# A decoder layer on one core: the value products moved to the end of each fused group, their copies to the start of the next, routing operands in PSUM, and two sums moved up

## The chip, the cores and the metric

The kernel runs on one core of a Trainium2 chip. It is written by hand for five engines that each work through their own instructions in order: TensorE (PE, matrix products and transposes), VectorE (DVE), ScalarE (ACT), GpSimd (POOL) and SyncE (SP, which here only issues transfers). An instruction starts when the one before it on its engine is through and the semaphores it waits for have been raised. The metric is the time on the device of one execution, in microseconds (us), median of several runs.

## The reference

Sixteen sequences of 256 tokens with 256 channels pass through a decoder layer with three residual blocks, each closed by a layer norm; all is float32.

```
x = _layernorm(x + attn(x, w_fc, w_proj, ln_g, ln_b))        # square of relu(scores), 4 heads
x = _layernorm(x + xattn(x, ctx, ctx, frac, ...))            # 16 heads of 16 channels
x = _layernorm(x + ffn(x, gate_W, gate_b, wi, wo, lora ...))

# xattn
logits = einsum('bhqd,bhkd->bhqk', Q, K) * scale
D = clip(frac[:, None, :] - frac[:, :, None], -0.2, 0.2)
attn = gamma * logits + delta * (ap * max(D, 0) + an * min(D, 0))
out = einsum('bhqk,bhkd->bhqd', softmax(attn), V) ; out @ Wo.T + bo

# ffn: one expert of eight per token, experts differ by a rank-4 addition
top1 = argmax(softmax(x @ gate_W.T + gate_b))
inter = relu(x @ wi.T + wi_b + (x @ lora_A[i].T) @ lora_B[i].T)    # i = top1
out = inter @ wo.T + wo_b
```

## The kernel before

The first 252 us are the first attention. Then the cross attention runs in N = 64 groups n: group n holds batch n//4 and four of its sixteen heads. The loop `for n in range(N + 2)` works on three groups at a time: `now` is group n, `last` is n-1, `older` is n-2. Its order of statements is the order on the engines; nothing rearranges it.

What a group goes through:

- `logits` (L664, PE): 32 products add the logits to the positive bias that ACT put into the four banks `ps_l` (`positive`, L654).
- `maxima` (L682, DVE): eight instructions add the negative bias, which POOL made (L642), and take each row's maximum.
- From n = 14 on the groups are *direct*: two of the four head blocks are exponentiated in place (`exp_rows`, L696, ACT), turned in 32x32 blocks by DVE (`blocks`, L707), written to DRAM (`away_z`) and read back in turned form into `pT` (`fetch`, L724). The other two have their maxima subtracted on POOL (`subtract`, L733), are turned by PE (`turned`, L743) and exponentiated by ACT (`exps`, L750).
- `attend` (L764, PE, 16 products) multiplies `pT` by the values, with a column of ones that gives the sums. It is done for `older`, two iterations after the logits. Two groups share one PSUM bank, `batch.av`, which is the single buffer of tag V in `psV` (`bufs=1`).
- `keep` (L777, DVE) copies that bank to `raw` when its second half is done, so for every other group; after every second copy `gather` lets SP issue the transfer of the sums (L574) and of the values (`away_v`, L579). `regroup` (L585), `invert` (reciprocal of the sums, L593), `spread` and `divide` follow one or two iterations on.

Each iteration also does one large piece and one small one of the projections: queries (L477), keys (L503), values (L532), output (L614), and the transposes of the next input (L464, `small_piece`, one iteration in four).

From n = FIRST = 15 on, the expert FFN of 512 earlier rows at a time is woven in: `tb, part = divmod(n - 15, 8)`, FUSED = 6 blocks of rows, so six cycles of eight parts. Part 0 turns the rows (L857, copies L860), part 1 computes the gates (L872, copy L882 on ACT), part 2 routes (`route`, L887 to L909, DVE) and parts 2 and 3 do the first FFN product (`inner`, L945) and the low-rank addition (`lora`, L958; L967 and L971 evict it), with `turn_um` (L919) in part 2. Parts 4 to 7 do the second product, one quarter each (`finish`: `outer`, L978, 16 products; then `add`, L991, and its statistics L191, L192, DVE). Parts 5 and 7 are called `apart`: their L978 goes into the bank of tag V, which the value products use too. So the products of parts 5 and 7 are left until the start of the part after, where 32 of them stand together behind the logits. In parts 2 and 3 (`halved`) the 16 products stand after `lora`.

`now.later` is true in parts 0 and 1, where the transposes of L707 are put off to the next part. `tile_b()` hands out three PSUM banks in turn (tags B, B, W); a transposition or product that takes a bank waits for the reader of what it held three hand-outs before.

Of the kernel before, what the change touches and what calls it, by code (L numbers as in the profile page):

```python
# [9 lines left out]
FP = mybir.dt.float32  # L10
AF = mybir.ActivationFunctionType
ALU = mybir.AluOpType
AX = mybir.AxisListType

P = 128
# [7 lines left out]
def tile_decoder_layer(ctx: ExitStack, tc: tile.TileContext, a: dict, out: bass.AP):  # L23


    nc = tc.nc
# [9 lines left out]
    E = a["gate_b"].shape[1]  # L36
# [9 lines left out]
    small = ctx.enter_context(tc.tile_pool(name="small", bufs=4))  # L46
# [3 lines left out]
    def tile_b():  # L50

        if turns:
            turns[0] += 1
            if turns[0] % 3 == 0:
                return psV.tile([P, 512], FP, tag="W", name="ps_b")
        return psB.tile([P, 512], FP, tag="B", name="ps_b")

    def tile_v(tag="V"):
        return psV.tile([P, 512], FP, tag=tag, name="ps_v")
# [6 lines left out]
    rev = const.tile([P, 4, E], FP, name="rev")  # L66
# [138 lines left out]
    def newton(mv, near, n):  # L205

        t = small.tile([P, n], FP, tag="sd", name="sd")
        nc.vector.scalar_tensor_tensor(t, mv[:, :, 1], EPS, near, ALU.add, ALU.mult)
        nc.vector.scalar_tensor_tensor(t, t, -0.5, near, ALU.mult, ALU.mult)
        rs = small.tile([P, n], FP, tag="rs", name="rs")  # L210
        nc.vector.scalar_tensor_tensor(rs, t, 1.5, near, ALU.add, ALU.mult)
        return rs
# [214 lines left out]
    if True:  # L427
# [357 lines left out]
        groups = [Group(batches[n // 4], n % 4) for n in range(4 * B)]  # L785
        N = len(groups)
# [19 lines left out]
        def step(piece):  # L806
            if piece:
                next(piece, None)
# [3 lines left out]
    if True:  # L812
        out_view = out.rearrange("(b j p) c -> b p j c", j=4, p=P)

        class Block:
# [68 lines left out]
            def route(self):  # L884
                ps = tile_b()
                for j in range(2):
                    nc.tensor.transpose(  # L887
                        ps[:, j * P : (j + 1) * P], self.gT[:, j * P : (j + 1) * P], ident
                    )

                gp = ps[:, 0 : 2 * P].rearrange("p (j t w) -> p t j w", j=2, t=2)
                lg = small.tile([P, 4, E], FP, tag="lg", name="lg")
                nc.vector.tensor_tensor(
                    lg.rearrange("p (t j) e -> p t j e", t=2), gp[:, :, :, 0:E],
                    gateb.rearrange("p (t j) e -> p t j e", t=2), ALU.add,
                )
                top = small.tile([P, 4, 1], FP, tag="top", name="top")
                nc.vector.tensor_reduce(top, lg, AX.X, ALU.max)

                hot = small.tile([P, 4, E], FP, tag="hot", name="hot")  # L900
                nc.vector.tensor_tensor(hot, lg, top.to_broadcast([P, 4, E]), ALU.is_ge)
                nc.vector.tensor_tensor(hot, hot, rev, ALU.mult)
                first = small.tile([P, 4, 1], FP, tag="first", name="first")
                nc.vector.tensor_reduce(first, hot, AX.X, ALU.max)
                nc.vector.tensor_tensor(hot, hot, first.to_broadcast([P, 4, E]), ALU.is_equal)

                self.um = small.tile([P, 4, 4, E, R], FP, tag="um", bufs=1, name="um")
                for j in range(4):
                    nc.vector.tensor_tensor(  # L909
                        self.um[:, j],  # L910
                        gp[:, j // 2, j % 2, E:W].rearrange("p (e r) -> p e r", r=R).unsqueeze(1).to_broadcast([P, 4, E, R]),
                        hot[:, j].unsqueeze(1).unsqueeze(3).to_broadcast([P, 4, E, R]),
                        ALU.mult,
                    )
# [98 lines left out]
    with tc.manual_schedule():  # L1013
# [15 lines left out]
        first = batches[0]  # L1029
# [8 lines left out]
        for tb in range(NB):  # L1038
# [16 lines left out]
            if tb > 2:  # L1055
                older = rows_in[tb - 3]
# [70 lines left out]
        FUSED, FIRST = NB - 2, 15  # L1127
# [26 lines left out]
        for n in range(N + 2):  # L1154
            now, nxt, last, older = (
                groups[n + d] if 0 <= n + d < N else None for d in (0, 1, -1, -2)
            )
            large_piece, small_piece, more = pieces(n)
            tb, part = divmod(n - FIRST, 8)
            ff = rows_out[tb] if 0 <= tb < FUSED or (tb == FUSED and part < 2) else None  # L1160
            halved = ff and part in (2, 3)
# [4 lines left out]
                done = rows_out[tb - 1]  # L1166

            apart = 0 <= tb < FUSED and part in (5, 7)
            b, og = divmod(n, 4)

            if n < 2:
# [7 lines left out]
                six.keep_gates()  # L1179
            if n > N:  # L1180
                six.inner(0, range(0, 1))
            if older and not halved and not apart and n != N:
                if 0 <= n - 1 - FIRST < 8 * FUSED and (n - 1 - FIRST) % 8 in (5, 7):
                    groups[n - 3].attend()
                older.attend()
            if last and last.direct:
                last.room()
                if not last.later:
                    last.fetch()
# [25 lines left out]
            if halved:  # L1215
                for g in range(2, 4) if last.direct else range(2):
                    last.turned(g)
                    last.exps(g)
                if part == 2:
                    ff.route()  # L1220
                if now.direct:
                    for g in range(2):
                        now.exp_rows(g)
                now.subtract((nc.gpsimd, nc.vector))
                if now.direct:
                    now.blocks()
                if part == 2:
                    ff.biased()
                if done:
                    done.ready(newton(done.mv, done.near, 4))  # L1230
                ff.inner(part - 2, range(0, 3))
                if part == 2:
                    ff.turn_um()
                ff.inner(part - 2, range(3, 4))
                ff.lora(part - 2, scalar=(0,))
                for g in range(4):
                    nxt.positive(g)
                older.attend()
            else:


                eager = n in (12, 13, 14)
                if n >= N or not now.direct:
                    acts = "e0 s0 s1 e1 s2 s3" if eager else "s0 s1 g e0 s2 e1 s3"
                    if ff and part == 0:
                        acts = "s0 s1 g e0 e1 s2"
                else:
                    acts = "s0 s1 g s2 s3" if last.direct else "s0 e0 s1 e1 s2 s3"
                    if part != 0 or not ff:
                        acts += " x0 x1"  # L1250
                for act in acts.split():
                    g = int(act[1:] or 0)
                    if act == "g":
                        if ff and part == 1 and n < N:
                            ff.keep_gates()
                    elif act[0] == "s":
                        if act == "s3" and n == N:
                            older.attend()
                        if nxt:
                            nxt.positive(g)  # L1260
                    elif act[0] == "x":
                        if now:
                            now.exp_rows(g)
                    elif last:
                        if last.direct:
                            g += 2
                        last.turned(g)
                        last.exps(g)
            if older:
                older.keep()  # L1270
            if n == 0:
                for piece in (outs[0], early[3], outs[1]):
# [25 lines left out]
                prep.rows()  # L1298
            if done and not halved:
                done.ready(newton(done.mv, done.near, 4))  # L1300
            if now and now.direct and not halved and not now.later:
                now.blocks()
            if ff and part >= 4:
                ff.finish(part - 4, tile_v() if apart else None)
            if last and (not last.direct or now and now.direct and not halved):
                for g in range(2, 4):
                    last.turned(g)
# [2 lines left out]
                step(large_piece)  # L1310
            step(small_piece)
            step(small_piece)
            if last and last.direct and last.later:
                last.fetch()
            if n == N:
# [117 lines left out]
```

## Time and profile before

| | |
|---|---|
| median of 3 runs | 887.87 us (887.59 to 888.99) |
| profiled execution | 887.49 us, span 885.7 us |
| granted TensorE clock | 0.999 |
| POOL busy | 466.6 us, 53% of the span |
| POOL waits (the longest in the loop): L733 for the maxima | 84.3 us, 40 waits |
| ACT, L967 for `lora` | 68.3 us, 16 waits |

"Span" is the time from the first to the last instruction that the profiler recorded; the rest of the execution lies around it. A line of the timeline gives the start of a run of like instructions, the time from the start of the first to the end of the last, the engine, the source line, the operation, what it writes and reads, the shape, how many there are, and in brackets the idle time just before, with what ended it. Busy times of consecutive matrix products overlap a little, as they are pipelined; from the start of one group to the start of the next is the truer length. In the chain of waits, each piece is followed back to what released it.

A cycle of eight parts takes some 77 us: the logits of part 1 start at 428.66, 506.48, 583.09, 659.71 and 736.33; the cycle that is looked at most closely here has its logits of parts 4 to 7 at 617.90, 627.16, 634.46 and 643.63 and of the following cycle's parts 0 to 3 at 650.93, 659.71, 666.36 and 680.90.

### The profile page before, as it was taken

To read this page: it belongs to the slowest core of one execution; us is meant where nothing else is said; L and a number is where in the kernel's file an instruction comes from. 1 tells how busy PE (TensorE), PEld (TensorE's weight loads), DVE (VectorE), ACT (ScalarE), POOL (GpSimd) and SP (SyncE) were. 2 spreads that over 40 slices of the span, in tenths; PEclk is the share of its full clock that TensorE was granted. 3 is DMA by queue.
4 is the path that set the end of the run, shared out by engine and by line. 5 is a ranking of instruction groups with operands and counts; after the bars stand their busy time and mean duration, and the time that the engine had idled before them with its cause. 6 is when DMAs were issued, how large, how long until landed. Compare 5 with 4: busy or idle time off the path is not lost.

```text
span 885.7 us, 20853 instructions
## 1 busy us (share of the span) xinstructions
PE 862.4 (97%) x7708; PEld 513.1 (58%) x7708; DVE 693.3 (78%) x1975; ACT 577.0 (65%) x1012; POOL 466.6 (53%) x455
## 2 busy tenths in 40 slices
PE   8999999999999999999999999999999999999997
PEld 4334444444456776567547656754765675576655
DVE  6878899889779898769778877877887787777444
ACT  5766777777788788647747765774875577475111
POOL 1100223322479898656828765883976678374010
PEclk9999999999999999999999999999999999999999
DMA  5501101010001333454454536445453644642001
GB/s 139 159 1 43 54 24 44 31 49 1 8 8 48 99 98 110 139 162 149 158 155 150 158 129 184 151 155 168 138 164 133 193 151 135 181 149 102 28 7 41
DMA packets 70373, 92.94 MB, mean 105 GB/s; under 512 B 13824, under 2 KB 55296, under 8 KB 70272
## 3 DMA queue, kind: packets, MB, share of 16 engines
q1 hardware_dynamic: 69696, 91.35, 33.2%
q8 instruction: 61, 1.00, 0.5%
q14 instruction: 40, 0.33, 0.1%
q10 hardware_dynamic: 576, 0.26, 0.1%
HBM read 50.43 MB, written 39.58 MB: 102 GB/s over the span
## 4 chain that ended last, share of the span: by engine, by line
PE 44%; DVE 11%; issue 2%; POOL 1%; ACT 1%; DMA 0%; ACTq 0%; POOLq 0%; DVEq 0%
PE ps_l L945 9%; PE ps_b L978 6%; PE ps_l L664 5%; PE ps_v L764 5%; PE ps_b L743 4%; DVE neg L682 3%; PE ps_b L614 3%; PE ps_v L978 3%; PE ps_b L477 2%; PE ps_l L958 2%; DVE z L707 1%; PE ps_b L503 1%; PE ps_b L532 1%; POOL neg L733 1%; DVE dpos L547 1%
## 5 line engine op out<-in xcount | busy, mean ns | idle before, releaser
L682 DVE CUSTOM_DVE_ANT_0 neg<-ps_l,neg 128x256 f32<-128x256 f32 x512 | 181.5, 420 | 41.4 <-PE ps_l L664 38.3
L642 POOL TENSOR_SCALAR neg<-dneg,aneg,delta 128x512 f32<-128x512 f32 x252 | 198.9, 804 | 20.9 <-PE ps_b L743 10.0
L654 ACT ACTIVATE ps_l<-dpos,apos_d 128x512 f32<-128x512 f32 x256 | 172.2, 688 | 49.9 <-DVE mx L682 30.9
L354 DVE TENSOR_TENSOR pr<-pr 128x1024 f32<-128x1024 f32 x128 | 153.8, 1243 | 30.2 <-ACT pr L353 29.8
L733 POOL TENSOR_TENSOR neg<-neg,mx 128x1024 f32<-128x1024 f32 x65 | 124.0, 1909 | 85.4 <-DVE mx L682 84.3
L353 ACT ACTIVATE pr<-ps_a 128x1024 f32<-128x1024 f32 x128 | 125.0, 1026 | 53.0 <-PE ps_a L345 52.7
L345 PE MATMUL ps_a<-xnT,kT 64*64 64x512 f32 x1024 | 124.6, 593 | 1.0 <-ACT xnT L330 0.4
L364 PE MATMUL ps_v<-pr,vv 64*64 64x512 f32 x1024 | 122.7, 589 | 0.0
L945 PE MATMUL ps_l<-xt,wi 128*128 128x512 f32 x248 | 111.7, 596 | 0.2
L750 ACT ACTIVATE pT<-ps_b 128x512 f32<-128x512 f32 x160 | 87.4, 590 | 32.4 <-PE ps_b L743 30.9
L743 PE MATMUL ps_b<-ident,neg 128*128 128x128 f32 x640 | 87.1, 277 | 3.4 <-ACT pT L750 2.3
L743 PEld LDWEIGHTS ps_b<-ident,neg 128*128 128x128 f32 x640 | 71.5, 141 | 24.0 <-issue 6.2
L364 PEld LDWEIGHTS ps_v<-pr,vv 64*64 64x64 f32 x1024 | 45.0, 133 | 64.5 <-issue 54.6
L379 POOL TENSOR_TENSOR xt<-xt,half 128x512 f32<-128x512 f32 x15 | 19.1, 1274 | 119.8 <-ACT half L378 119.8
L419 POOL TENSOR_TENSOR hid<-hid,bo 128x256 f32<-128x256 f32 x32 | 43.6, 1366 | 71.8 <-ACT hid L251 71.8
L696 ACT ACTIVATE neg<-neg,mx 128x256 f32<-128x256 f32 x192 | 81.3, 498 | 0.0
L764 PE MATMUL ps_v<-pT,vaug 128*32 128x256 f32 x1024 | 74.3, 385 | 7.2 <-DVE x L991 6.0
L664 PE MATMUL ps_l<-kM,qT 32*64 32x256 f32 x2048 | 79.8, 388 | 0.0
L345 PEld LDWEIGHTS ps_a<-xnT,kT 64*64 64x64 f32 x1024 | 41.9, 133 | 65.3 <-issue 52.5
L945 PEld LDWEIGHTS ps_l<-xt,wi 128*128 128x128 f32 x248 | 45.6, 191 | 49.4 <-issue 44.6
L978 PE MATMUL ps_b<-wof,hT 128*128 128x256 f32 x304 | 68.4, 380 | 0.0
L524 POOL TENSOR_SCALAR kM<-keys,of_head 128x512 f32<-128x512 f32 x22 | 38.7, 1760 | 48.4 <-DVE keys L513 48.4
(137 smaller groups left out, 1183.3 us busy)
## 6 DMA issues: line engine op xcount, KB each, us to landing
pT<-away_z SPq DMA_DIRECT2D x192, 128.0 KB
away_z<-z SPq DMA_DIRECT2D x24, 512.0 KB
away_z<-kT SPq DMA_DIRECT2D x24, 512.0 KB
away_v<-raw SPq DMA_DIRECT2D x16, 512.0 KB
cT<-in_ctxT SPq DMA_DIRECT2D x16, 256.0 KB
v<-away_v SPq DMA_DIRECT2D x32, 128.0 KB
invs<-rows SPq DMA_DIRECT2D x16, 256.0 KB
x<-in_x SPq DMA_DIRECT2D x7, 512.0 KB
```

The source lines that it names most:

```text
L345: nc.tensor.matmul(sc[64 * k : 64 * k + 64, h, :], lhsT=kT[64 * h : 64 * h + 64, q, hf * P + 64 * k : hf * P + 64 * k + 64], rhs=self.xnT[ ...
L353: nc.scalar.activation(pr, sc, AF.Relu)
L354: nc.vector.tensor_tensor(pr, pr, pr, ALU.mult)
L364: nc.tensor.matmul(self.acc[k][64 * h : 64 * h + 64, :], lhsT=vv[64 * k : 64 * k + 64, hf, 64 * q : 64 * q + 64], rhs=pr[64 * k : 64 * k + ...
L642: nc.gpsimd.tensor_scalar(self.neg[:, g], self.batch.dneg, aneg[:, h : h + 1], delta, ALU.mult, ALU.mult,)
L654: nc.scalar.activation(banks[g], self.batch.dpos.rearrange("p j k -> p (j k)"), AF.Copy, scale=apos_d[:, h : h + 1],)
L664: nc.tensor.matmul(banks[g][64 * h : 64 * h + 64, j * S : (j + 1) * S], lhsT=self.batch.qT[rows, self.o, j * P + 64 * h : j * P + 64 * h + ...
L682: nc.vector.tensor_tensor_reduce(out=self.t[:, g, j, :], in0=banks[g][:, j * S : (j + 1) * S], in1=self.neg[:, g, j, :], scale=-1.0 if min ...
L733: eng.tensor_tensor(rows, rows, top.to_broadcast([P, 4, S]), ALU.subtract)
L743: nc.tensor.transpose(ps[:, k * S + j * P : k * S + (j + 1) * P], self.t[:, g, j, k * P : (k + 1) * P], ident,)
L945: nc.tensor.matmul(self.banks[g], lhsT=wi[:, c, f * P : (f + 1) * P], rhs=self.xT[:, c, :], start=(c == 0), stop=False,)
L978: nc.tensor.matmul(ps[:, 0:C], lhsT=self.hT[f][:, j * P : (j + 1) * P], rhs=wof[:, f, :], start=(f == 0), stop=(f == FC - 1),)
```

## The change

- **Values last.** For n = 15 to 63, `older.attend()` no longer stands behind the logits (or behind `lora` in parts 2 and 3): it is the last thing of the iteration, after the large and the small piece. Putting off the products of parts 5 and 7 to the following part falls away.
- **Copies first.** `keep` of those groups goes to the start of the following iteration, behind the logits and before the maxima, the fetch and the regrouping: `groups[n - 3].keep()`.
- **Some sums first.** In parts 5 and 7 `ff.finish`, with its addition and statistics on DVE, stands ahead of `now.blocks()`, the transposition on DVE.
- **Routing operands in PSUM.** `lg` and the intermediate masks (`held`) lie in free columns of the bank that the gates were turned into; only the final mask `hot` lies in SBUF. The number of instructions of each engine stays the same.

```diff
                 gp = ps[:, 0 : 2 * P].rearrange("p (j t w) -> p t j w", j=2, t=2)
-                lg = small.tile([P, 4, E], FP, tag="lg", name="lg")
+                lg = ps[:, 2 * P : 2 * P + 4 * E].rearrange("p (j e) -> p j e", e=E)
+                held = ps[:, 3 * P : 3 * P + 4 * E].rearrange("p (j e) -> p j e", e=E)
...
-                nc.vector.tensor_tensor(hot, lg, top.to_broadcast([P, 4, E]), ALU.is_ge)
-                nc.vector.tensor_tensor(hot, hot, rev, ALU.mult)
+                nc.vector.tensor_tensor(held, lg, top.to_broadcast([P, 4, E]), ALU.is_ge)
+                nc.vector.tensor_tensor(held, held, rev, ALU.mult)
                 first = small.tile([P, 4, 1], FP, tag="first", name="first")
-                nc.vector.tensor_reduce(first, hot, AX.X, ALU.max)
-                nc.vector.tensor_tensor(hot, hot, first.to_broadcast([P, 4, E]), ALU.is_equal)
+                nc.vector.tensor_reduce(first, held, AX.X, ALU.max)
+                nc.vector.tensor_tensor(hot, held, first.to_broadcast([P, 4, E]), ALU.is_equal)
...
             apart = 0 <= tb < FUSED and part in (5, 7)
+            lastly = FIRST <= n < N
...
-            if older and not halved and not apart and n != N:
-                if 0 <= n - 1 - FIRST < 8 * FUSED and (n - 1 - FIRST) % 8 in (5, 7):
-                    groups[n - 3].attend()
+            if older and not lastly and n != N:
                 older.attend()
+            if FIRST < n <= N:
+                groups[n - 3].keep()
             if last and last.direct:
...
                 ff.lora(part - 2, scalar=(0,))
                 for g in range(4):
                     nxt.positive(g)
-                older.attend()
...
-            if older:
+            if older and not lastly:
                 older.keep()
...
+            if apart:
+                ff.finish(part - 4, tile_v())
             if now and now.direct and not halved and not now.later:
                 now.blocks()
-            if ff and part >= 4:
-                ff.finish(part - 4, tile_v() if apart else None)
+            if ff and part >= 4 and not apart:
+                ff.finish(part - 4)
...
             step(small_piece)
             step(small_piece)
+            if lastly:
+                older.attend()
             if last and last.direct and last.later:
                 last.fetch()
```

The lines of the kernel after are those of the kernel before plus one from L893 on, and shifted by a few more in the loop.

## The prediction

> **What bounds the kernel now.** I read the busy times first, then the list of waits, then the timelines of single engines in one cycle.
>
> ```profile
> PE 862.4 (97%) x7708; PEld 513.1 (58%) x7708; DVE 693.3 (78%) x1975; ACT 577.0 (65%) x1012; POOL 466.6 (53%) x455
> ```
>
> PE is the bound on average, with 3% idle. So values that only change places gain at most the places where PE waits, and they lose wherever they were filling a wait. The waits with a value product behind them are short:
>
> ```profile
> PEld ps_v L764 <- DVE x L991: 11.1, 12, 2.1
> ...
> PE ps_v L764 <- DVE x L991: 6.0, 6, 1.6
> ```
>
> Six waits of PE on the sum L991 make 6.0 us, about one per cycle, in part 0:
>
> ```profile
> 649.96 1.04 PE L743 MATMUL ps_b<-ident,neg 128*128 128x128 f32 x8
> 650.93 1.12 PE L664 MATMUL ps_l<-kM,qT 32*64 32x256 f32 x32
> 652.83 2.65 PE L764 MATMUL ps_v<-pT,vaug 128*32 128x256 f32 x32 [0.78 <-DVE x L991]
> ```
>
> Here 32 products wait 0.78 us and then take 2.65 us where part 6's take 1.86 (635.51 to 637.38), the second half waiting for ACT's exponentials: 0.78 + 0.79, about 1.5 us of idle PE. Part 1 has 1.87 for 16 products where 1.00 is usual (0.8 idle), part 2 has 0.52 before L919. Together 2.8 us a cycle. The sum L991 is late because DVE is full in parts 6 and 7; its timeline there has no gap over 0.4 us from 635.91 on:
>
> ```profile
> 648.62 1.72 DVE L547 CUSTOM_DVE_ANT_1 dpos<-frow,nfcol 128x512 f32<-128x512 f32 x1
> ...
> 651.14 0.16 DVE L246 SCALAR_TENSOR_TENSOR nm<-mv,rs 128x4 f32<-128x4 f32 x1
> 651.22 1.25 DVE L707 STREAM_TRANSPOSE z<-neg 128x1024 f32<-128x1024 f32 x1
> 652.39 0.38 DVE L991 TENSOR_TENSOR x<-x,ps_v 128x256 f32<-128x256 f32 x1
> ```
>
> In part 4 the end is set by ACT, while PE has the values to do:
>
> ```profile
> 619.43 1.07 PE L764 MATMUL ps_v<-pT,vaug 128*32 128x256 f32 x16
> 620.43 1.99 PE L532 MATMUL ps_b<-wv,cT 128*128 128x256 f32 x8
> 622.26 3.62 PE L978 MATMUL ps_b<-wof,hT 128*128 128x256 f32 x16
> 625.72 1.04 PE L743 MATMUL ps_b<-ident,neg 128*128 128x128 f32 x8
> 626.59 0.64 PE L464 MATMUL ps_b<-ident,hid 128*128 128x128 f32 x4
> 627.16 1.12 PE L664 MATMUL ps_l<-kM,qT 32*64 32x256 f32 x32
> ...
> 620.55 2.76 ACT L654 ACTIVATE ps_l<-dpos,apos_d 128x512 f32<-128x512 f32 x4 [2.21 <-PE ps_v L764]
> 623.25 1.69 ACT L696 ACTIVATE neg<-neg,mx 128x256 f32<-128x256 f32 x4
> 624.84 0.59 ACT L251 ACTIVATE hid<-hid,nm,rs 128x256 f32<-128x256 f32 x1
> 626.35 1.08 ACT L750 ACTIVATE pT<-ps_b 128x512 f32<-128x512 f32 x2 [0.92 <-PE ps_b L743]
> ```
>
> ACT is free at 625.43 and waits 0.92 us for the transposes; PE hardly waits.
>
> **The change, part by part.** Everything is a replay by hand of the cycle shown, each instruction with the duration it has there, in the order and with the waits of the program after.
>
> *Part 4.* The values (1.00) leave the front, so L532 starts at 619.43, L978 at 621.26, L743 at 624.72 and ends at 625.6. L464 takes the third bank in turn, which the second exponential reads. ACT's chain does not move: it starts from the maxima, which start from the logits, and is free for L750 at 625.43; its two end at 626.5. L464 (0.53 of PE time) runs to 627.0, the values 1.00 to 628.03: that is when part 5's logits start, instead of 627.16, **+0.87**. PE has 0.9 us of new idle time, which the values covered. Lower bound: 0, if L464 started right behind L743 (625.6); upper bound: if the exponentials end where they do now (627.44), 628.97, +1.8. I take 0.87. L464 stands in part 4 of five cycles.
>
> *Parts 5 and 6.* The sum L991 now precedes the transposition L707 on DVE, so part 5's values find their bank free at once: the logits of part 6 start at 635.46 with 16 values already done (+1.0, then -1.0 within part 6, since all products are only moved). But maxima of part 6 start 0.84 later (636.74). The copy (0.69) leaves this stretch, 638.67, yet little is won by it: L547 behind it takes 1.33 us because it ends with POOL's L733, which starts when the maxima end, and L547 takes 0.68 where POOL does nothing. DVE's stretch ends at 645.4 instead of 644.6.
>
> *Part 7.* The copy comes first here: 645.35 to 646.05, maxima from 646.0 (before: 644.91). Behind: the reciprocal, keys, L547 held by POOL's L733 until about 651.3, the four small steps to 652.3, the sum L991 to 652.7. PE itself is through with L978 and L743 at 651.07; the values want the bank that L991 reads, and so wait from 651.07 to 652.75. They end at 653.75, when the logits of part 0 start, instead of 650.93: +2.8. Queued behind this wait on PE are those logits, and behind them all of part 0. On SP the sums and `away_v` go out 1.3 us before the fetch (its 4 issues 1.74) and the regrouping waits for `away_v` to land (4.3 us from issue to landing: 641.78 to 646.04); the sums take 2.6 us and land near 648.7, just when the reciprocal's turn comes. Price 0; if they are late, all they are late by, up to 0.6.
>
> *Part 0.* The 32 products and their waits are gone (650.93 to 655.41 was 4.48 for 1.05 of logits). Maxima from 655.03, ACT's positives to 658.68 (+0.9 behind the maxima, 2.76 long), then ACT's copies L860 to 659.7. PE is ready for L464 before, but its bank waits for the second copy: 659.8 to 660.3, values to 661.3. That is part 1's logits: **+1.6** (before: 659.71).
>
> *Parts 1 and 2.* The 0.8 of part 1 is won: part 2's logits at 667.17 (+0.8). L945 starts at 669.55 (+1.0). The routing, from DVE's L893 to L905, takes 2.4 us now, with two-operand steps stretched by POOL's L865:
>
> ```profile
> 671.60 0.15 DVE L893 TENSOR_TENSOR lg<-ps_b,gateb 128x32 f32<-128x32 f32 x1
> 671.78 0.18 DVE L898 TENSOR_REDUCE top<-lg 128x4 f32<-128x32 f32 x1
> 672.00 0.60 DVE L901 TENSOR_TENSOR hot<-lg,top 128x32 f32<-128x32 f32 x1
> 672.64 0.65 DVE L902 TENSOR_TENSOR hot<-hot,rev 128x32 f32<-128x32 f32 x1
> ```
>
> L893, with one operand in PSUM, takes 0.15. With L901, L902 and L905 (0.43) at 0.15 to 0.2 each, some 1.2 us go. Then L919 starts behind L945 without its 0.52 wait: 669.55 + 5.32 = 674.87 against 674.45, **+0.42** per crossing. If the operands bring nothing, the wait stays and it is +0.9. The trace has 0.19 for L901 with POOL idle, so below 0.15 each there is nothing to expect.
>
> [...]
>
> *Sum.* Five crossings, five parts 4: 5 x (0.87 + 0.42) = 6.45. First cycle, whose part 0 loses a filled wait before any gain from part 7: +0.5 (bounds 0 and 0.87). Last crossing, where no L464 stands behind and PE waits 1.63 us for L991: -0.3 (bounds -1.6 and 0). +6.6 on the profiled 887.49 is 894.1; the median lies 0.4 above that execution. I predict 894.0.
> With all bounds: part 4 from 0 to +1.8, crossing from -0.5 (the gain at L919 stays, the rest is regained in part 0) to +1.6, so 5 x -0.5 - 1.6 = -4 to 5 x 3.4 + 0.9 = +18; halfway to each, the likeliest case's own range is 889 to 899.
>
> **Rivals.**
> 1. *The waits go, and nothing takes their place* (faster). Place: parts 7 to 2. It decides if L991 of part 7 ends before 651.07, when PE is ready. For it: L991 is 1.25 earlier relative to L707. Against it: the maxima before it start 1.1 later and L547 is held by POOL. Price: all 2.8 us in six cycles give -17, 871; with part 4's loss of 4.4 it is 875. If only part 7's crossing comes out even and the routing's 0.52 goes in each of six cycles, 884.8. Chance 0.24; I see it between 875 and 886.
> 2. *Even* (no change). Part 4's +0.87 is taken up by DVE's slack (1.24 us idle before the maxima at 628.44) and the crossing gives +-0.4. Against: PE has no slack behind part 4. 886 to 889.7, chance 0.11.
> 3. *SP falls behind* (slower still). The regrouping at the head of part 7 holds SP until `away_v` has landed; if the turned blocks of part 7 go out behind it, the values of part 1 wait. From an SP delay of about 2 us on it shows, some 0.6 to 1.5 us a cycle: 897 to 903. Against: away_z of part 7 follows L707, at 654. Chance 0.10.
> My forecast: 0.55.
>
> A measurement of this kernel can tell 0.2%, 1.8 us, from no change. Faster 0.24, same 0.11, slower 0.65. The range 882.5 to 900 leaves out the deep end of rival 1 and half of rival 3.
>
> **What would show it.** Right: PE's wait before L764 on L991 (part 7) grows to some 1.7 us while those of part 0 go; part 4 shows 0.9 idle before L464; no wait on L909 before L919; L901, L902 near 0.2. The cycle is 77.9 instead of 76.6. Wrong: the cycle at or below 76.6; L991 in part 7 done before the transposes end; or new waits on the fetched `pT`, which I priced at nothing.

## The result and the profile after

| | median | against the kernel before |
|---|---|---|
| kernel before | 887.73 us (887.58 to 888.99, 4 runs) | |
| kernel after | 894.42 us (893.47 to 894.87, 4 runs) | 1.0065, 95% interval 1.0053 to 1.0078 |
| profiled execution after | 894.21 us, span 892.5 us | span 6.8 us longer |

The forecast was 894.0. The busy times of the page are nearly those of before (PE 858.5 instead of 862.4 us), so the kernel after has no more work to do; PE stands still longer. The list of waits of the kernel after says where (engine, tile and line that waits, what it waits for: total us, times, longest):

```profile
PEld ps_v L764 <- DVE x L992: 11.5, 6, 2.3
...
PE ps_v L764 <- DVE x L992: 9.9, 6, 2.0
...
PE ps_b L743 <- DVE vaug L540: 6.4, 6, 2.1
...
PE ps_b L464 <- ACT pT L750: 3.8, 5, 0.9
```

The waits on the sum (now L992) have not gone but grown from 6.0 to 9.9 us, and two new ones have come. The 2.6 us before the transposes of um are off the list. How long each part of a cycle takes, from its logits to those of the next part, in the same two executions (n is the group, the third cycle from n = 35 on; all by the starts of L664 on PE's timeline):

| part (n) | 4 (35) | 5 (36) | 6 (37) | 7 (38) | 0 (39) | 1 (40) | 2 (41) | 3 (42) | sum |
|---|---|---|---|---|---|---|---|---|---|
| before | 9.26 | 7.30 | 9.16 | 7.30 | 8.79 | 6.65 | 14.53 | 13.62 | 76.61 |
| after | 10.18 | 8.30 | 8.30 | 9.89 | 7.57 | 5.86 | 13.61 | 13.63 | 77.34 |

The cycle with part 4's logits at 621.89 shows the two places. PE's timeline in part 4:

```profile
628.71 1.04 PE L743 MATMUL ps_b<-ident,neg 128*128 128x128 f32 x8
630.49 0.66 PE L464 MATMUL ps_b<-ident,hid 128*128 128x128 f32 x4 [0.74 <-ACT pT L750]
631.08 1.07 PE L764 MATMUL ps_v<-pT,vaug 128*32 128x256 f32 x16
632.08 1.12 PE L664 MATMUL ps_l<-kM,qT 32*64 32x256 f32 x32
```

and ACT's:

```profile
628.84 0.59 ACT L251 ACTIVATE hid<-hid,nm,rs 128x256 f32<-128x256 f32 x1
629.35 1.08 ACT L750 ACTIVATE pT<-ps_b 128x512 f32<-128x512 f32 x2
```

PE has finished L743 and stands until ACT's second exponential has let go of the bank; the values, which had covered this, stand behind. Part 7 on PE, on DVE and on POOL:

```profile
651.56 3.62 PE L979 MATMUL ps_v<-wof,hT 128*128 128x256 f32 x16
655.01 1.04 PE L743 MATMUL ps_b<-ident,neg 128*128 128x128 f32 x8
657.56 1.07 PE L764 MATMUL ps_v<-pT,vaug 128*32 128x256 f32 x16 [1.52 <-DVE x L992]
658.57 1.12 PE L664 MATMUL ps_l<-kM,qT 32*64 32x256 f32 x32
...
654.50 1.72 DVE L547 CUSTOM_DVE_ANT_1 dpos<-frow,nfcol 128x512 f32<-128x512 f32 x1
...
657.10 0.41 DVE L992 TENSOR_TENSOR x<-x,ps_v 128x256 f32<-128x256 f32 x1
...
653.77 1.90 POOL L733 TENSOR_TENSOR neg<-neg,mx 128x1024 f32<-128x1024 f32 x1 [2.52 <-DVE mx L682]
```

1.52 us of wait for L992, with the logits queued behind it. And the routing on DVE, whose rows stood at 0.60 and 0.65 before:

```profile
677.24 0.17 DVE L894 TENSOR_TENSOR ps_b<-ps_b,gateb 128x32 f32<-128x32 f32 x1
...
677.67 0.20 DVE L902 TENSOR_TENSOR ps_b<-ps_b,top 128x32 f32<-128x32 f32 x1
677.90 0.20 DVE L903 TENSOR_TENSOR ps_b<-ps_b,rev 128x32 f32<-128x32 f32 x1
```

One thing was not foreseen at all. In the first two cycles the wait of part 7 is 2.04 us, and the windows of the kernel after show what follows (stretch, length, then busy us and instructions of PE, PEld, DVE, ACT and POOL, then the granted TensorE clock, DMA share, GB/s):

```profile
418.00:420.00 2.00, 1.94 (x13) 1.52 (x12) 1.59 (x6) 2.00 (x6) 1.81 (x1) 1.00 0.94 291
420.00:422.00 2.00, 0.02 (x3) 0.02 (x4) 1.86 (x7) 0.84 (x3) 2.00 (x2) 1.00 0.60 133
422.00:424.00 2.00, 2.00 (x32) 1.00 (x40) 1.71 (x3) 2.00 (x5) 2.00 (x4) 0.69 0.29 89
424.00:426.00 2.00, 2.00 (x26) 1.09 (x11) 0.68 (x3) 0.67 (x2) 1.07 (x2) 0.50 0.73 294
426.00:428.00 2.00, 2.00 (x13) 1.71 (x13) 2.00 (x13) 1.78 (x3) 0.00 (x0) 0.96 0.03 9
```

Behind an idle stretch from 420 to 422 the clock goes to 0.50, and it is back, at 0.96, in the stretch from 426 on; the logits in between take 2.01 us where 1.12 is usual.

### The profile page after: what moved, and what is told of

Read it like the earlier page. It is cut to its first block, busy times and chain, and to the rows that moved or that the text cites. A ratio compares the mean times of both kernels' runs of the same rounds, so it can differ in the third digit from the quotient of the medians.

```text
span 892.5 us, 20853 instructions
## 1 busy us (share of the span) xinstructions
PE 858.5 (96%) x7708; PEld 510.1 (57%) x7708; DVE 687.5 (77%) x1975; ACT 577.9 (65%) x1012; POOL 466.4 (52%) x455
## 4 chain that ended last, share of the span: by engine, by line
PE 36%; DVE 12%; issue 4%; DMA 3%; POOL 2%; ACT 2%; SPq 1%; POOLq 0%; DVEq 0%
PE ps_l L946 9%; PE ps_l L664 5%; PE ps_v L764 4%; PE ps_b L979 4%; DVE neg L682 4%; PE ps_b L743 3%; PE ps_v L979 3%; PE ps_b L477 2%; PE ps_b L614 2%; DMA away_z<-z 2%; PE ps_l L959 1%; DVE dneg L547 1%; POOL neg L642 1%; DVE st L191 1%; ACT neg L696 1%
## 5 line engine op out<-in xcount | busy, mean ns | idle before, releaser
L654 ACT ACTIVATE ps_l<-dpos,apos_d 128x512 f32<-128x512 f32 x256 | 172.2, 688 | 77.9 <-DVE mx L682 65.3
L733 POOL TENSOR_TENSOR neg<-neg,mx 128x1024 f32<-128x1024 f32 x65 | 124.0, 1909 | 105.2 <-DVE mx L682 101.2
L743 PE MATMUL ps_b<-ident,neg 128*128 128x128 f32 x640 | 88.7, 277 | 9.7 <-DVE vaug L540 6.4
L743 PEld LDWEIGHTS ps_b<-ident,neg 128*128 128x128 f32 x640 | 71.4, 141 | 31.9 <-issue 12.8
L664 PE MATMUL ps_l<-kM,qT 32*64 32x256 f32 x2048 | 81.3, 395 | 0.0
L764 PE MATMUL ps_v<-pT,vaug 128*32 128x256 f32 x1024 | 69.6, 390 | 11.3 <-DVE x L992 9.9
L972 DVE TENSOR_SCALAR hT<-ps_l,wib 128x512 f32<-128x512 f32 x43 | 29.8, 745 | 43.6 <-PE ps_l L959 43.6
```

Of the source, the lines that this page charges most:

```text
L654: nc.scalar.activation(banks[g], self.batch.dpos.rearrange("p j k -> p (j k)"), AF.Copy, scale=apos_d[:, h : h + 1],)
L664: nc.tensor.matmul(banks[g][64 * h : 64 * h + 64, j * S : (j + 1) * S], lhsT=self.batch.qT[rows, self.o, j * P + 64 * h : j * P + 64 * h + ...
L733: eng.tensor_tensor(rows, rows, top.to_broadcast([P, 4, S]), ALU.subtract)
L743: nc.tensor.transpose(ps[:, k * S + j * P : k * S + (j + 1) * P], self.t[:, g, j, k * P : (k + 1) * P], ident,)
```

## The experiments

The theory at the start: part 4 lays bare ACT's exponentials, part 7 a chain on DVE; routing in PSUM wins; the rest only moves. The line numbers in an experiment's kernel are those of the kernel after, but for a few lines in the loop. "Off the kernel after" compares medians.

**1. The routing alone**, on the kernel before: only the hunk in `route`.

```diff
+                lg = ps[:, 2 * P : 2 * P + 4 * E].rearrange("p (j e) -> p j e", e=E)
+                held = ps[:, 3 * P : 3 * P + 4 * E].rearrange("p (j e) -> p j e", e=E)
...
+                nc.vector.tensor_tensor(held, lg, top.to_broadcast([P, 4, E]), ALU.is_ge)
```

> The kernel before, with only the routing's operands moved to PSUM. Theory (each of five or six crossings wins 0.52 us at the transposes of um, or 0.9 us as the cycles of the kernel after suggest: logits of part 2 to logits of part 3 take 13.61 instead of 14.53 us): faster by 3 to 5.5 us, 882.3 to 884.9. Rival A (what is won before the transposes of um is waited for again before the logits of part 3, for ACT's positives): 887 to 888, no change. Rival B (the routing is only quicker where the values have moved too): 887.

882.99 us, ratio 0.9944 (0.9932 to 0.9957). Part 2 takes 13.61 us in each cycle from the second on, and every other part what it took before, within 0.13; the gain stays to the end. It is 0.92 a cycle, not 0.52: from the first product L945 to the first transpose of um 5.20 instead of 5.89 us, and from there to the next product 0.43 instead of 0.67, so a second, shorter wait between the four transposes has gone as well.

**2. Part 4's values back behind the logits**, on the kernel after:

```diff
+            front = lastly and ff and part in (4,)
...
-            if older and not lastly and n != N:
+            if older and (not lastly or front) and n != N:
                 older.attend()
...
-            if lastly:
+            if lastly and not front:
                 older.attend()
```

> The kernel after, with the values of part 4 alone back behind the logits. Theory (they filled the wait for ACT's exponentials before the transposes L464, 0.9 us in each of five cycles): 4.4 to 4.7 us faster than the kernel after, about 889.8. Rival (DVE's start of part 5 has slack that takes it up, so the cost appears again in part 5 to 7): less than 2 us faster than the kernel after.

888.81 us, ratio to before 1.0002 (0.9993 to 1.0011), so 5.6 off the kernel after. Part 4 takes 9.26 again, every other part as in the kernel after but where the clock falls: by the starts of the logits, the five parts 4 differ by 4.74 us together, a little over the 4.4 to 4.7 expected. That the medians differ by more goes with the clock: this run's executions at a granted clock of 0.999 took 886.7 to 887.3, those at 0.997 888.8 to 889.0, and the one at 0.995 890.1, which is 4.1 and 4.5 below the two of the kernel after at 0.995. The slack that the rival saw on DVE in part 5 takes nothing back.

**3. The reciprocal behind the sum** in part 7, on the kernel after:

```diff
-            if inverse:
+            if inverse and not apart:
                 inverse.invert()
...
             if apart:
                 ff.finish(part - 4, tile_v())
+                if inverse:
+                    inverse.invert()
```

> The kernel after, with the reciprocal of part 7 moved behind the sum L992. It removes from DVE's path the 0.27 us of the reciprocal and, in the first two cycles, its wait of 0.41 and 0.45 us for the gathered sums. Theory (the waits of PE before part 7's values are 2.04 us there and 1.52 in the others; only behind the two of 2.04 does the granted clock fall to 0.5): no fall of the clock, 0.3 us won in each of five crossings and about 1.5 to 2 more in each of the first two, 889.5 to 891.5. Rival A (the fall of the clock does not hang on that wait): the clock still falls, 892 to 893. Rival B (the reciprocal is not on the path): 894.

893.8 us: a miss for the theory, and rival B's time. PE's waits are unchanged within 0.01 us (2.04 in two cycles, 1.52 in three), although DVE had one instruction less, and no waiting for the gathered sums, ahead of L992. So neither the reciprocal nor the late sums are on the path. The clock did not fall behind the two waits of 2.04 in this execution and did behind one of 2.06 at 347 us.

**4. The sums not first**, on the kernel after: the transposition L707 ahead of L992 in parts 5 and 7, as before.

```diff
-            if apart:
-                ff.finish(part - 4, tile_v())
             if now and now.direct and not halved and not now.later:
                 now.blocks()
-            if ff and part >= 4 and not apart:
-                ff.finish(part - 4)
+            if ff and part >= 4:
+                ff.finish(part - 4, tile_v() if apart else None)
```

> The kernel after, with the transposition L707 ahead of the sums again in parts 5 and 7, as before. Theory (values at the end of parts 5 and 7 wait for L992): PE's wait in part 7 grows by 1.25 us, from 1.5 to 2.8, in part 5 a wait of about 0.8 us arises, and behind waits of that length the granted clock falls each time: 905 to 915. Rival A (no fall of the clock): 900 to 905. Rival B (DVE's order is taken up elsewhere): 894 to 896.

911.06 us, ratio 1.0264 (1.025 to 1.0278). PE waits 2.65 or 3.17 us in part 7, part 5 takes 9.20 instead of 8.30, and the clock falls five times in the loop, three of them behind the five waits of part 7, so not each time as expected. With the values at the end of the part this order is needed.

**5. Part 7's values behind the logits of part 0**, on the kernel after:

```diff
+            if FIRST < n <= N and ((n - 1 - FIRST) % 8 == 7):
+                groups[n - 3].attend()
...
-            if lastly:
+            if lastly and not (ff and part == 7):
                 older.attend()
```

> The kernel after, with the values of part 7 behind the logits of part 0 instead of at the end of part 7. Theory (the logits need not wait for the sum L992, but the part's end hangs on DVE, whose maxima start when the transposition L707 ends): the logits of part 0 start 2.5 us earlier, those of part 1 only 0.5 us earlier in each of five crossings, and PE's wait shrinks to some 0.4 us, so that the granted clock does not fall behind it: 887.5 to 890. Rival (PE's queue is the price, and what PE regains in part 0 is kept): 1.5 us or more in each crossing, 881 to 885.

886.99 us, ratio 0.9996 (0.9987 to 1.0005), 7.4 off the kernel after and 0.5 below the range of the theory. Part 7 takes 7.30 as before, but part 0 9.53: 16.83 together, 0.63 less than the kernel after and still 0.75 more than before; what makes up this 0.75 no run isolates. The logits come 2.6 us earlier and nearly 2.0 of it is given back within part 0, where DVE and ACT set the end. In the first two cycles 1.7 and 2.2 us are won, as the clock no longer falls there; another 2.4 are won in the tail, at n = 62.

**6. Sums first and routing, without moving the values**, on the kernel before: the edits of run 1 and the last one of run 4 the other way round.

> The kernel before, with the routing's operands in PSUM and the sums of parts 5 and 7 ahead of the transposition L707, the values and copies where they were. Theory (the second half of the 32 products of part 0 waits for ACT's exponentials, which end as before, so the first half's earlier start is given back): the same as the routing alone, 882 to 884. Rival (the wait of 0.78 us for L991 in part 0 is the price of the order, and goes): 877.5 to 879.5.

881.47 us, ratio 0.9935 (0.9922 to 0.9949). Parts 7 and 0 take 16.08 together as before, so in the cycles the order of the sums is worth nothing there (single parts at n = 16 and 56 even lose 0.6 and 0.2). What is won against run 1 stands in one place, n = 61 in the tail, which takes 9.35 instead of 10.86: the wait of 1.63 us on L991 that the kernel before had at 786.6. The medians lie 1.5 us apart, the two profiled executions only 0.6. The result is 0.5 below the range of the theory, which had no term for the tail.

**7. L547 behind the sum** in part 7, on the kernel after:

```diff
-            if now and now.direct:
+            if now and now.direct and not (apart and part == 7):
                 rest_of(n)
...
             if apart:
                 ff.finish(part - 4, tile_v())
+                if part == 7:
+                    rest_of(n)
```

> The kernel after, with part 7's L547 moved behind the sum L992 on DVE. Theory (L547 ends with POOL's L733, whatever stands before it, and the small steps and L992 stand behind it; that is why the late reciprocal won nothing): L992 ends some 1.5 us earlier, PE's wait before part 7's values goes from 1.5 and 2.0 to under 0.5 us, maxima and logits follow by 1.0 to 1.5 us in each of five crossings, and the granted clock does not fall behind that wait: 884.5 to 889. Rival (it is the late maxima alone, and L547 only runs in time that is waited out anyway): 892 to 894.5.

891.89 us, ratio 1.0042 (1.003 to 1.0055): a miss in time and a partial one in the waits. PE's wait falls to 1.08 and 1.60, not under 0.5. DVE's and POOL's timelines of this run show why. DVE:

```profile
652.04 0.78 DVE L513 TENSOR_SCALAR keys<-ps_b,bk 128x256 f32<-128x256 f32 x2
652.74 1.18 DVE L208 SCALAR_TENSOR_TENSOR sd<-mv,near 128x4 f32<-128x4 f32 x1
653.96 0.62 DVE L209 SCALAR_TENSOR_TENSOR sd<-sd,near 128x4 f32<-128x4 f32 x1
```

POOL:

```profile
652.01 1.89 POOL L733 TENSOR_TENSOR neg<-neg,mx 128x1024 f32<-128x1024 f32 x1 [2.54 <-DVE mx L682]
```

L208 took 0.15 us when it stood behind L547. It takes 1.18 now and ends when POOL's L733 ends, at 653.9. It has inherited the stall: the next instruction with two operands in SBUF stands still in place of L547. This would also explain run 3, where L547 came earlier and ended no sooner.

**8. The sum ahead of L547 and of the small steps**, on the kernel after:

```diff
+            if apart and part == 7:
+                ff.finish(part - 4, tile_v())
             if now and now.direct:
                 rest_of(n)
...
-            if apart:
+            if apart and part == 5:
                 ff.finish(part - 4, tile_v())
```

> The kernel after, with part 7's sum L992 and its statistics ahead of L547 and of the small steps of the scaling too. Theory (DVE's instructions with two operands in SBUF stand still until POOL's L733 ends; L992, with one operand in PSUM, does not, so it runs in time that was waited out): L992 ends when its product does, near 655.4 in the cycle whose part 7 logits start at 648.68, PE's wait before part 7's values falls under 0.2 us in every cycle, and part 0 plus part 7 take 16.5 instead of 17.46 us; 888 to 890, with no fall of the clock but behind the wait near 347 us. Rival (L992 is held by the late maxima or by POOL like the others): PE still waits over 0.8 us, 892 to 894.

891.91 us, ratio 1.0051 (1.0038 to 1.0064). The mechanism is as stated: L992, with one operand in PSUM, takes 0.42 us from 653.53 while L733 runs from 652.09 to 653.99, and PE goes from L743 to the values without a wait. The time is not: the timelines of this run have PE's wait in pieces in part 0, and ACT's behind the small steps.

```profile
654.29 1.07 PE L764 MATMUL ps_v<-pT,vaug 128*32 128x256 f32 x16
...
658.93 1.14 PE L857 MATMUL ps_b<-ident,x 128*128 128x128 f32 x8 [0.59 <-ACT pT L750]
660.92 0.63 PE L743 MATMUL ps_b<-ident,neg 128*128 128x128 f32 x4 [0.86 <-DVE vaug L540]
662.34 0.65 PE L743 MATMUL ps_b<-ident,neg 128*128 128x128 f32 x4 [0.79 <-ACT xt L860]
...
656.32 2.07 ACT L251 ACTIVATE x<-hid,nm,rs 128x256 f32<-128x256 f32 x4 [1.96 <-DVE nm L246]
```

Counted from the logits of part 7, the small steps end 0.8 us later now; ACT's L251, which waits for them, starts 9.33 instead of 8.53 us behind these logits, and ACT's exponentials and copies come late. Parts 7 and 0 take 17.41 against 17.46. Rival and theory both missed this: the part has two chains of nearly the same length, through L992 and through the scaling.

**9. Both places at once**, on the kernel after: the edits of runs 2 and 5.

> The kernel after, with the values of part 4 behind their logits and those of part 7 behind the logits of part 0: the edits of the runs part-4-front and part-7-behind together. Theory (the two places are separate and make up the loss): their gains add, 5.6 and 7.4 us off 894.4, 881 to 882.5; what is left of the values at the end then costs nothing against the routing alone (883.0). Rival (the second repair finds part of its gain already taken, since both move the same DVE work): 884 to 887.

882.81 us, ratio 0.9943 (0.9929 to 0.9957). 11.6 off the kernel after, of 13.0 if the two added fully, between the ranges of theory and rival, and within 0.2 us of the routing alone. So the two places, with the falls of the clock behind part 7's wait, make up the loss.

**10. Values last in part 1 only**, on the kernel of run 6:

```diff
+            behind = FIRST <= n < N and part == 1
-            if older and not halved and not apart and n != N:
+            if older and not halved and not apart and not behind and n != N:
...
             step(small_piece)
             step(small_piece)
+            if behind:
+                older.attend()
```

> The kernel of the run sums-and-route (routing in PSUM, sums first, values and copies as before), with the values of part 1 alone at the end of their part. Theory (part 1 is the one place where the values at the end take away a wait, for ACT's exponentials, without laying one on the part behind: logits of part 1 to logits of part 2 take 5.86 instead of 6.65 us): 0.8 us in each of six cycles, 1.2 in the first, 876 to 877.5. Rival (what part 1 wins is waited for before the first FFN product or the routing of part 2): 880.5 to 881.5.

877.93 us, ratio 0.9893 (0.9881 to 0.9906): faster than both kernels, and 0.4 short of the forecast. Part 1 takes 6.19 instead of 6.65, 0.46 won where 0.79 was expected; parts 2 and 3 keep all of it.

Copies at their old place with the values at the end were not tried: the regrouping in the same iteration reads what they gather, so this takes more than one edit.

## Why the prediction was right, and where its terms were off

The direction and the two places are right: run 2 shows the one in part 4, run 5 the one in part 7. That the sum came so close, +6.7 on the profiled executions where +6.6 was predicted, is luck in part: a cycle without a fall of the clock takes 77.34 us, not the 77.9 of the forecast, and the clock, which the forecast had nowhere, supplied what was missing. (The forecast's own sum also gives 894.1 + 0.4 = 894.5 for the median, not the 894.0 that it states.) Summed by the starts of the logits, relative to those of n = 14 (which came 0.4 us earlier in the kernel after, ahead of anything that was changed), the terms do not all agree:

| term | predicted | measured |
|---|---|---|
| five parts 4 | +4.35 | +4.4 |
| five crossings (parts 5 to 3) | +2.1 | +1.8 |
| first cycle, parts 0 to 3 | +0.5 | -0.2 |
| from n = 60 on | -0.3 | +1.2 |

*Part 4* was right within 0.05 us: 0.92 against 0.87 in the three middle cycles (0.59 in the first, 1.04 in the last), shown by run 2, which takes away this term and no other.

*Parts 5 and 6*: +1.0 and -0.86, as replayed. *Part 7*: relative to part 5's logits, part 0's come 2.73 later against the 2.8 of the replay, with PE's wait at 1.52 against 1.68; runs 4, 5 and 8 each move this wait in the direction that the replay gives. What held L992 was called "L547 held by POOL's L733"; run 7 shows that this was one step too specific, since L208 in its place stood still just as well. L547 also does not end with L733, as the replay of part 6 has it: it ends 0.54 us behind (641.34 against 640.80 before), where it takes 0.68 alone, so it stands until L733 is through and does most of its own work then. *Part 0*: -1.21, as replayed; that its end hangs on DVE and ACT, not on PE, is shown by run 5. I named ACT's copies as the last release there; the profile after has PE wait 0.96 us on DVE's L540 first, the end is the same.

*Part 2 is the term that was mis-sized.* From part 2's logits to part 3's the replay won 0.38 us (+0.8 to +0.42); 0.92 came, as run 1 shows. The replay put L945 2.38 us behind the logits where both kernels have 2.20, and it had L919 5.32 behind L945 where 5.19 came. The shorter wait between the transposes of um, another 0.23, it left out. So a normal crossing was worth -0.2 us, not +0.42: three of the five measure that. The replay also named L865 alone as what stretches the routing; L901 ended when L733 did (672.60 and 672.57), and L865 ran beside the later steps.

The steps themselves came at the 0.15 to 0.2 us that the prediction took for each with an operand in PSUM: L902 and L903 take 0.20 us and L906 0.19, where L901, the step that is now L902, took 0.19 in SBUF with POOL idle.

*The clock made up for it.* In the first two crossings part 7's wait is 2.04 us because part 6 carries small work of the last 1024 rows on DVE in these cycles, which I had left out: at n = 21 two instructions of their statistics (0.6 us), at n = 29 the four steps of their scaling, which end in 2.3 us, one of them held beside L733 for 1.75. There the crossings measure +1.1 and +1.2. In run 3, where the clock held behind the same two waits, they measure +0.1 and -0.4: the falls cost 1.1 and 1.6 us, 2.7 together. No rival of the prediction had this. Taking these 2.7 off the +6.7, an estimate, leaves some +4 without the falls, still inside the range of 889 to 899 but not within 0.4 us of the forecast.

*The tail* went the other way: the wait on L992 went at n = 61, as assumed, but 1.32 and 1.38 us came in at 806 and 815, the second for a copy that now stands first in a part in which DVE is late.

Of the rivals, the first ("the waits go") holds for parts 1 and 2 alone; its point of decision, L991 of part 7 done before PE is ready, was not reached. The second had the normal crossing right (-0.2, inside its +-0.4) and part 4 wrong, as run 2 shows. The third, SP falling behind, did not come: DVE waited 0.41 and 0.45 us for the sums in two cycles, and run 3 shows that this cost nothing.

## What to carry to other kernels

Work without a deadline that stands at the front of a stage may be what fills a wait there; before it is moved to the end, look for the chain on another engine that ends at the same time, and move it only where it waits itself at the front. Here that was part 1, 0.46 us a cycle by run 10; in parts 4 and 7 it cost, and the other parts were not tried one by one. A product that shares a PSUM bank with a sum on another engine makes the next stage's first instruction wait for that sum when it stands ahead of it: 1.52 to 2.04 us here; in run 5 it waits behind these logits, for 0.46 to 0.99. And when an instruction is stretched by a neighbour engine, moving it away did not help while what took its place read the same way (run 7, where L208 took 1.18 us instead of 0.15).

## What was not expected of the hardware

**The granted clock falls after waits of some 2 us, but not always.** Over the profiled executions of the kernel after and of the seven experiments on it, PE stood idle 14 times for 2.04 to 2.08 us; the clock went to 0.5 for 3.41 us behind nine of them, and the same wait at 347 us was followed by a fall in some executions and in others not. Of five waits of 2.33 to 2.66 us two were followed by one, of two of 3.17 both; single waits of up to 1.63 us never were. In run 8 a fall came behind several shorter waits in a row, the longest 1.03 us. A fall at n = 15 costs 1.5 us (parts 0 and 1 together 16.6 instead of 15.1).

The traces show when a fall comes. Within one execution, the starts of the falls lie whole multiples of 3.413 us apart (in run 4, the four behind the first come 22, 46, 70 and 134 times 3.413 us after it; in the kernel after, the second comes 23 times 3.413 us after the first, in run 2 44 times). Counted off from its falls, the time of each of these executions divides into cells of 3.413 us, and every fall begins at the end of one. Adding up PE's waits inside each cell separates the cases nearly without exception: all 14 falls in the loops of these eight executions follow a cell with 1.79 to 3.16 us of waiting, and of the cells that no fall followed one had 1.85 us and the rest at most 1.78. A wait of 2.04 us that lies in one cell (419.94 to 421.98 in the kernel after, in the cell that ends at 422.75) is followed by a fall. The same wait cut by the end of a cell (in run 3: 421.47 to 423.51, at most 1.16 us of it in one cell) is not. In run 8, several shorter waits made up 1.89 us in one cell.

**DVE instructions with two SBUF operands stand still beside POOL's L733 and L865.** L547 took 0.68 us alone and 1.72 beside L733, L208 0.15 and, beside L733, 1.18 (run 7); the routing's steps beside L733 and L865 took 0.19 to 0.20 with an operand in PSUM (L902, L903 and L906 of the kernel after) and 0.60, 0.65 and 0.43 without (L901, L902 and L905 before). Beside POOL's L524 the stall varied: L208 took 0.15 and L209 0.46 there in the kernel after. L992, with one operand in PSUM, took 0.42 beside L733 (run 8) and 0.41 to 0.42 in the kernel after.
